# Bringing the experts' outputs to the tokens: 64-row products per batch, or 128-row products for two batches at once

## The chip, the cores and the metric

The kernel runs on one core of one Trainium2 chip. A core has a matrix engine (TensorE, shown as PE for products and PEld for weight loads), a vector engine (VectorE, DVE), a scalar engine (ScalarE, ACT), GpSimd (POOL), and DMA queues, of which SyncE's (SP) carries most transfers here. The metric is device time in microseconds (us); before the change it is 4524.53 us, the median of three runs (4481.02, 4524.53 and 4561.62). A profile of one further execution is at hand.

## The reference

The input `x` has 4 batches of 128 channels x 64 x 64 places. Four layers follow one another. Layer 0 is a state-space layer, layer 1 a hypergraph layer on the pairwise distances of 4096 places. Layers 2 and 3 treat the places as 4096 tokens of 128 channels, and each consists of an attention (linear and causal in layer 2, windowed without softmax in layer 3) and a feed-forward part with 64 experts. The change concerns the end of this feed-forward part, which occurs twice:

```
logits = einsum('bsd,ed->bse', x, gate_w) + gate_b
probs  = softmax(logits, axis=1)                  # over the 4096 tokens, per expert
vals, idx = top_k(probs over tokens, 8)           # each expert picks 8 tokens per batch
pooled = sum of the 8 picked tokens, weighted by vals      # (batch, expert, 128)
out    = expert MLP(pooled)                       # 128 -> 512 -> 128, own weights per expert
outputs[b, idx] += out[b, e] * vals               # back to the picked tokens
t = t + outputs
```

Each expert has one output row per batch, and this row, times the token's probability, is added to each of its eight tokens. Written as matrices, outputs of batch b = routeᵀ (4096 tokens x 64 experts) times the experts' outputs (64 x 128), where `route` holds the probabilities of the picked tokens and zero elsewhere.

## The kernel before

All arrays are fp32 in the parts concerned. `X` (128 partitions x 4 batches x 32 blocks x 128 channels) stays on the chip from the end of layer 1: a partition is a token's place within a block of 128 tokens. `Net.ffn` is called as the second half of layer 2, with `out=None`, and as the second half of layer 3, with the output tensor.

Within `ffn` two batches are handled together as a pair `p` (0 or 1): partitions 0 to 63 hold the 64 experts of batch 2p, partitions 64 to 127 those of batch 2p+1. So `route[p]` is 128 rows x 4096 tokens, `dens[p]` is one divisor per row, and `outT` holds all experts' outputs with channels in the partitions. The stages, in order:

1. Gate: layernorm of the tokens, transposes, logits (L970, L973, L976), and for each pair the eight largest logits per row, the exponentials and `route` (L980 to L990).
2. Pooling by products with the transposed `route` (L997 to L1011).
3. Experts, four at a time, sixteen groups: weights arrive over SP's queue in transfers of 1 MB (L947, L950) into a ring of two, products L1025, L1027, L1035, L1040, and the turn of the outputs L1048, L1049.
4. The experts' outputs are turned so that experts are in the partitions (L1057), the last layer's bias is added (L1059) and the softmax's divisor is applied (L1060). The result is `ob`, 128 rows x 128 channels, one for each pair.
5. The outputs are brought to the tokens. The loops run over the pair p, the chunk c of 512 tokens and the half r, that is the batch 2p+r.

In step 5 the call of layer 2 makes, for each (p, c, r), four products (L1071). In each, the weights are `route[p][rows, 128 tokens]` and the moving operand is `obs[p][rows, :]`, where `rows` are the 64 rows of the half r. The four results fill one PSUM tile of 128 x 512, and VectorE adds it to `X` (L1072). The call of layer 3 works the other way round, since the output has channels in the partitions. For each (p, c, r) four products with the identity (L1078) turn `X` into a PSUM tile of 128 channels x 512 tokens, and a fifth (L1082), with `obs[p][rows, :]` as weights and `route[p][rows, 512 tokens]` moving, adds the experts' part to it. ScalarE (r = 0) or VectorE (r = 1) copies the tile (L1087), and SP stores it (L1088).

The PSUM tiles of step 5 carry the tag `ps` in a pool with two buffers for each tag, so two of them exist at a time. `ob` comes from the pool `wp` with one buffer for each tag. Each engine runs its own instructions in order; a scheduler has put them in order when the kernel was built, and semaphores join the engines. After the first `ffn` comes `attn3`, which starts with layernorm statistics of `X` (L700 and L705 to L712), loads Wq, Wk and Wv (L845) and turns them (L846), and works with products of 128 rows throughout (L867, L870, L876, L896, L905).

Of the kernel before, what the change touches and what calls it, by code (L numbers as in the profile page):

```python
# [7 lines left out]
F32 = mybir.dt.float32  # L8
# [3 lines left out]
ALU = mybir.AluOpType  # L12
# [4 lines left out]
P = 128  # L17
# [6 lines left out]
E = 64  # L24
# [14 lines left out]
class Net:  # L39
# [871 lines left out]
    def ffn(self, name, out=None):  # L911
# [4 lines left out]
        nc, tc, a, X = self.nc, self.tc, self.a, self.X  # L916
# [3 lines left out]
        with ExitStack() as ctx:  # L920
            wp = ctx.enter_context(tc.tile_pool(name="fw", bufs=1))
# [4 lines left out]
            ps = ctx.enter_context(tc.tile_pool(name="fps", bufs=2, space=PSUM))  # L926
# [7 lines left out]
            b2 = wp.tile([P, P], F32, tag="b2", name="b2")  # L934
# [20 lines left out]
            route, dens = [], []  # L955
            for p in range(B // 2):
                lg = big.tile([P, N], F32, tag="lg", name="lg")
                zs = [[big.tile([P, 4, P], F32, tag="z", name="zf", bufs=17) for r in range(2)] for c in range(NCH)]
                for c in range(NCH):
                    pl = ps.tile([P, CH], F32, tag="ps", name="ps_l")  # L960
                    for r in range(2):
# [4 lines left out]
                        pt = ps.tile([P, 4, P], F32, tag="tr", name="ps_t")  # L966
                        for i in range(4):
                            j = 4 * c + i
# [25 lines left out]
                for c in range(NCH):  # L994
                    pt = ps.tile([P, 4, P], F32, tag="tr", name="ps_rt")
# [4 lines left out]
                    for i in range(4):  # L1000
                        j = 4 * c + i
                        for r in range(2):
                            nc.tensor.matmul(  # L1003
                                pp[r * E : (r + 1) * E, :], rt[:, i, r * E : (r + 1) * E], zs[c][r][:, i, :],
                                start=j == 0, stop=j == NB - 1,
# [3 lines left out]
                pt = ps.tile([P, P], F32, tag="tr", name="ps_pt")  # L1009
# [9 lines left out]
            for q in range(NG // 4):  # L1019
                po = aps.tile([P, 4, P], F32, tag="acc", name="ps_eo")  # L1020
                for k in range(4):
# [4 lines left out]
                    for i in range(EG):  # L1026
                        nc.tensor.matmul(  # L1027
                            ph[i * M : (i + 1) * M, :], pooled[:, (g * EG + i) * B : (g * EG + i) * B + M], w1[:, i, :],
                            start=False, stop=True, skip_group_check=True,
# [3 lines left out]
                    pt = ps.tile([P, 4, P], F32, tag="tr", name="ps_hT")  # L1033
# [4 lines left out]
                    for c in range(4):  # L1038
                        for i in range(EG):
                            nc.tensor.matmul(  # L1040
                                po[i * M : (i + 1) * M, k, :], hT[:, c, i * M : (i + 1) * M], w2[:, i, c, :],
                                start=c == 0, stop=c == 3, skip_group_check=True,
# [3 lines left out]
                pt = ps.tile([P, 4, P], F32, tag="tr", name="ps_oT")  # L1046
# [7 lines left out]
            obs = []  # L1054
            for p in range(B // 2):
                pt = ps.tile([P, P], F32, tag="tr", name="ps_ot")
                nc.tensor.transpose(pt, outT[:, 2 * p : 2 * p + 2, :].rearrange("p b e -> p (b e)"), self.ident)  # L1057
                ob = wp.tile([P, P], F32, tag=f"ob{p}", name="ob")
                nc.vector.tensor_tensor(ob, pt, b2, ALU.add)  # L1059
                nc.vector.tensor_scalar(ob, ob, dens[p], None, ALU.mult)  # L1060
                obs.append(ob)
            for p in range(B // 2):
                for c in range(NCH):
                    for r in range(2):
                        b, rows = 2 * p + r, slice(r * E, (r + 1) * E)
                        x = X[:, b, 4 * c : 4 * c + 4, :]
                        if out is None:
                            po = ps.tile([P, 4, P], F32, tag="ps", name="ps_f")
                            for i in range(4):
                                cs = slice((4 * c + i) * P, (4 * c + i + 1) * P)  # L1070
                                nc.tensor.matmul(po[:, i, :], route[p][rows, cs], obs[p][rows, :], start=True, stop=True)  # L1071
                            nc.vector.tensor_tensor(x, x, po, ALU.add)  # L1072
                        else:

                            sl = slice(c * CH, (c + 1) * CH)
                            po = ps.tile([P, CH], F32, tag="ps", name="ps_f")
                            for i in range(4):
                                nc.tensor.matmul(  # L1078
                                    po[:, i * P : (i + 1) * P], x[:, i, :], self.ident,
                                    start=i == 0, stop=False, skip_group_check=True,  # L1080
                                )
                            nc.tensor.matmul(  # L1082
                                po, obs[p][rows, :], route[p][rows, sl], start=False, stop=True,
                                skip_group_check=True,
                            )
                            o = tp.tile([P, CH], F32, tag="s", name="of")
                            (nc.vector.tensor_copy if r else nc.scalar.copy)(o, po)  # L1087
                            nc.sync.dma_start(out[b, :, sl], o)  # L1088
# [62 lines left out]
```

## Time and profile before

| | us |
|---|---|
| median of three runs | 4524.53 |
| the profiled execution | 4506.08 |
| its span | 4504.3 |
| layers 0 and 1, to the last stretch with the scan (0 to 2860) | 2860 |
| rest of layer 1, and attention of layer 2 (2860 to 3695) | 835 |
| first ffn: gate and pooling (3695 to 3825) | 130 |
| first ffn: experts (3825 to 3917.8) | 92.8 |
| first ffn: outputs to the tokens (3917.8 to 3964.5) | 46.7 |
| attention of layer 3 (3964.5 to 4195) | 230.5 |
| second ffn: gate and pooling (4195 to 4327) | 132 |
| second ffn: experts (4327 to 4434.2) | 107.2 |
| second ffn: outputs to the tokens, and the store (4434.2 to 4504.3) | 70.1 |

Over the span PE is busy for 82%, VectorE for 69%, GpSimd for 54%, ScalarE for 44%. These are averages over stages that are limited by different engines. A product in fp32 leaves two records on PE, each with its own weight load on PEld. A record's duration includes the time in which the next one is already running, so the sum of durations is more than the busy time, and the step from one start to the next is what a stream of products costs. "64*128" ahead of a shape says that the product uses 64 rows and 128 columns of the array. PEclk is the clock that TensorE was granted, as a share of the full one. In a list of groups the figures after the bar are busy time, mean duration of one in ns, the idle time of the engine just before, and what ended that idle time.

### The profile page before, as it was taken

What the parts mean: (1) busy time and instruction counts of PE and PEld (TensorE: products, weight loads), DVE (VectorE), ACT (ScalarE), POOL (GpSimd) and SP (SyncE); (2) the same over time, 40 slices, a digit from 0 to 9 for tenths busy, and PEclk for the clock granted to TensorE, in tenths of its full rate; (3) what the DMA queues carried; (4) which work ended last, traced back from release to release, by engine and by line L of the source; (5) the groups of instructions that cost most, each with busy time, mean ns of one, the idle gap of its engine ahead of it and who ended that gap; (6) DMA issues with size and microseconds to landing.
All of it is one profiled execution on the core that took longest, in us unless ns stands there. A gap on an engine that the chain in (4) does not pass through costs nothing. (4 is left out here: it accounts for less than half of the span.)

```text
span 4504.3 us, 50176 instructions
## 1 busy us (share of the span) xinstructions
PE 3713.7 (82%) x17975; PEld 2095.2 (47%) x17975; DVE 3124.2 (69%) x5140; ACT 1981.6 (44%) x3104; POOL 2415.8 (54%) x1182
## 2 busy tenths in 40 slices
PE   6887768888887888887878888899977995899778
PEld 2333233345433434543434454456535763578435
DVE  5888889997668999666999866453118985287621
ACT  4655554456445445644544564213225643022221
POOL 5999889887777888677888877300021000000000
PEclk8988878999998899998889999999988997789878
DMA  3455544454464445455455535312250000800044
GB/s 102 155 150 150 143 114 139 124 148 132 126 189 114 125 130 154 122 151 164 113 132 138 153 107 169 119 61 77 76 200 31 1 2 6 297 2 1 2 172 166
DMA packets 261741, 524.36 MB, mean 116 GB/s; under 512 B 21706, under 2 KB 24306, under 8 KB 261490
## 3 DMA queue, kind: packets, MB, share of 16 engines
q1 hardware_dynamic: 250194, 501.78, 37.9%
q10 hardware_dynamic: 11296, 19.37, 1.3%
q8 instruction: 142, 2.33, 0.2%
q14 instruction: 109, 0.89, 0.1%
HBM read 443.47 MB, written 77.59 MB: 116 GB/s over the span
## 5 line engine op out<-in xcount | busy, mean ns | idle before, releaser
L284 POOL TENSOR_TENSOR db<-dx,bt 128x1024 f32<-128x1024 f32 x512 | 1203.0, 2353 | 331.7 <-DVE hs L302 214.6
L302 DVE TENSOR_TENSOR_SCAN hs<-hs,carry,db 128x512 f32<-128x512 f32 x812 | 1035.2, 1282 | 177.5 <-ACT hs L296 95.2
L296 ACT ACTIVATE hs<-dl,A 128x512 f32<-128x512 f32 x1024 | 706.6, 692 | 740.6 <-DVE ho L312 687.1
L497 PE MATMUL ps_g<-xn 128*128 128x512 f32 x1152 | 602.5, 654 | 99.8 <-DVE inc L500 74.3
L319 POOL TENSOR_TENSOR ho_s<-ho_s,ho 128x1024 f32<-128x1024 f32 x288 | 677.1, 2351 | 13.8 <-DVE ho L312 13.1
L312 DVE TENSOR_TENSOR ho<-hs,bt 128x1024 f32<-128x1024 f32 x464 | 563.2, 1214 | 1.6
L520 PE MATMUL ps_ed<-xs,inc 128*128 128x258 f16 x4096 | 513.6, 286 | 18.3 <-ACT inc L513 8.6
L520 PEld LDWEIGHTS <-inc 128*128 128x128 fp8e4 x4096 | 417.8, 102 | 134.6 <-issue 60.6
L500 DVE SCALAR_TENSOR_TENSOR inc<-ps_g,hcl,hb 128x512 fp8e4<-128x512 f32 x576 | 420.3, 736 | 36.7 <-PE ps_g L497 20.9
L497 PEld LDWEIGHTS ps_g<-xn 128*128 128x128 f32 x1152 | 216.0, 204 | 416.6 <-DVE inc L500 182.9
L340 PE MATMUL ps_y<-ho,cst 128*128 128x512 f32 x512 | 274.0, 678 | 108.9 <-POOL ho L308 91.5
L620 PE MATMUL ps_v<-inc_v,es 128*128 128x512 fp8e4 x1536 | 343.1, 383 | 19.2 <-DMA bt<-bcd 17.3
L620 PEld LDWEIGHTS <-es 128*128 128x128 f16 x2048 | 202.7, 99 | 288.9 <-issue 64.1
L513 ACT CAST inc<-ps_t 128x512 fp8e4<-128x512 f32 x448 | 232.1, 600 | 94.5 <-PE ps_t L509 94.3
L222 PE MATMUL ps_c<-xt,wc 128*128 128x512 f32 x512 | 234.9, 613 | 12.6 <-DVE inc L500 6.8
L340 PEld LDWEIGHTS ps_y<-ho,cst 128*128 128x128 f32 x512 | 105.1, 214 | 269.0 <-POOL ho L308 122.6
L526 ACT COPY ed<-ps_ed 128x129 f32<-128x129 f32 x128 | 34.0, 266 | 383.7 <-PE ps_ed L520 383.7
L527 DVE TENSOR_TENSOR ed<-ps_ed,ed 128x129 f32<-128x129 f32 x128 | 36.6, 286 | 211.8 <-ACT ed L526 208.8
L302 DVE TENSOR_TENSOR_SCAN hs<-hs,db 128x512 f32<-128x512 f32 x116 | 141.2, 1223 | 53.6 <-POOL db L284 42.6
L536 POOL TENSOR_TENSOR ed<-ed,rdeg 128x512 f32<-128x512 f32 x32 | 33.3, 1039 | 250.7 <-DVE rdeg L532 250.7
L222 PEld LDWEIGHTS ps_c<-xt,wc 128*128 128x128 f32 x512 | 99.8, 198 | 140.2 <-issue 119.2
L509 PE MATMUL ps_t<-ident,strip 128*128 128x128 fp8e4 x1344 | 115.1, 227 | 51.4 <-ACT inc L513 16.9
(262 smaller groups left out, 5785.5 us busy)
## 6 DMA issues: line engine op xcount, KB each, us to landing
bt<-bcd SPq DMA_DIRECT2D x512, 512.0 KB
inc<-inc SPq DMA_DIRECT2D x192, 256.0 KB
inc_v<-inc SPq DMA_DIRECT2D x96, 512.0 KB
w<-in_L_ffn_weight SPq DMA_DIRECT2D x32, 1024.0 KB
w2f<-in_L_ffn_weight SPq DMA_DIRECT2D x32, 1024.0 KB
strip<-inc SPq DMA_DIRECT2D x84, 256.0 KB
x<-x ACTq DMA_DIRECT2D x32, 256.0 KB
xn<-x SPq DMA_DIRECT2D x32, 256.0 KB
```

The costliest lines, as they stand in the source:

```text
L222: nc.tensor.matmul(s["ps"][h], wc[:, h, j, :], xt[:, j : j + T], start=j == 0, stop=j == 3)
L284: nc.gpsimd.tensor_tensor(db, s["dx"], bc(s["bt", n][:, 0, :], 2), ALU.mult)
L296: act(nc.scalar.activation(hs[:, k, :], s["dl"][:, k, :], AF.Exp, scale=A[:, k, n : n + 1]))
L302: nc.vector.tensor_tensor_scan(to[:, h, :], hs[:, h, :], db[:, h, :], init, ALU.mult, ALU.add)
L312: nc.vector.tensor_tensor(ho, hs, ct, ALU.mult)
L319: nc.gpsimd.tensor_tensor(s["sum", n // G], s["sum", n // G], ho, ALU.add)
L340: nc.tensor.matmul(s["y"][h], self.ident, t[:, h, :], start=False, stop=n == DS - 1 and k == len(terms) - 1,)
L497: nc.tensor.matmul(pq, xn[v // 4][:, v % 4 * P : (v % 4 + 1) * P], xn[c], start=True, stop=True)
L500: nc.vector.scalar_tensor_tensor(inc[:, v, :], pq, hc[:, v : v + 1], hb, ALU.subtract, ALU.is_gt, saturate=False)
L513: later(1, lambda: act(nc.scalar.copy(inc[:, v, :], pt, saturate=False)))
L520: nc.tensor.matmul(pe[:, : 2 * P + 2], inc[:, v, i * P : (i + 1) * P], xs[:, v, :], start=v == 0, stop=v == NB - 1,)
L620: nc.tensor.matmul(pv, es[:, e, k, :], inc[:, e, :], start=e == 0 and k == 0, stop=e == NB - 1 and k == 1,)
```

## The change

`ob` becomes twice as wide: 128 rows x 2 x 128. Its two column blocks belong to the two batches of the pair. Rows 0 to 63 are filled in block 0 only and rows 64 to 127 in block 1 only; GpSimd sets the tile to zero first. The bias and the divisor are applied to each half by instructions of 64 rows.

In the call of layer 2 each product now takes all 128 rows of `route[p]` for 128 tokens as weights and the whole `ob` (256 columns) as moving operand, so that it yields both batches of the pair side by side; the zeros keep the batches apart. A PSUM tile holds 2 blocks of tokens x 2 batches x 128 channels, and one addition on VectorE adds it to `X` of both batches. In the call of layer 3 the fifth product takes block r of `ob` with all 128 rows as weights and all 128 rows of `route[p]` moving; the rows of the other batch meet zeros. The names of the lines behind the change move by seven: L1088 becomes L1095, for example.

```diff
             for p in range(B // 2):
                 pt = ps.tile([P, P], F32, tag="tr", name="ps_ot")
                 nc.tensor.transpose(pt, outT[:, 2 * p : 2 * p + 2, :].rearrange("p b e -> p (b e)"), self.ident)
-                ob = wp.tile([P, P], F32, tag=f"ob{p}", name="ob")
-                nc.vector.tensor_tensor(ob, pt, b2, ALU.add)
-                nc.vector.tensor_scalar(ob, ob, dens[p], None, ALU.mult)
+                ob = wp.tile([P, 2, P], F32, tag=f"ob{p}", name="ob")
+                nc.gpsimd.memset(ob, 0.0)
+                for r in range(2):
+                    rows = slice(r * E, (r + 1) * E)
+                    nc.vector.tensor_tensor(ob[rows, r, :], pt[rows, :], b2[rows, :], ALU.add)
+                    nc.vector.tensor_scalar(ob[rows, r, :], ob[rows, r, :], dens[p][rows, :], None, ALU.mult)
                 obs.append(ob)
             for p in range(B // 2):
                 for c in range(NCH):
                     for r in range(2):
-                        b, rows = 2 * p + r, slice(r * E, (r + 1) * E)
-                        x = X[:, b, 4 * c : 4 * c + 4, :]
                         if out is None:
-                            po = ps.tile([P, 4, P], F32, tag="ps", name="ps_f")
-                            for i in range(4):
-                                cs = slice((4 * c + i) * P, (4 * c + i + 1) * P)
-                                nc.tensor.matmul(po[:, i, :], route[p][rows, cs], obs[p][rows, :], start=True, stop=True)
+                            j = 4 * c + 2 * r
+                            po = ps.tile([P, 2, 2, P], F32, tag="ps", name="ps_f")
+                            for i in range(2):
+                                nc.tensor.matmul(
+                                    po[:, i, :, :].rearrange("p r c -> p (r c)"), route[p][:, (j + i) * P : (j + i + 1) * P],
+                                    obs[p].rearrange("p r c -> p (r c)"), start=True, stop=True,
+                                )
+                            x = X[:, 2 * p : 2 * p + 2, j : j + 2, :].rearrange("p r i c -> p i r c")
                             nc.vector.tensor_tensor(x, x, po, ALU.add)
                         else:
+                            b = 2 * p + r
                             sl = slice(c * CH, (c + 1) * CH)
                             po = ps.tile([P, CH], F32, tag="ps", name="ps_f")
                             for i in range(4):
                                 nc.tensor.matmul(
-                                    po[:, i * P : (i + 1) * P], x[:, i, :], self.ident,
+                                    po[:, i * P : (i + 1) * P], X[:, b, 4 * c + i, :], self.ident,
                                     start=i == 0, stop=False, skip_group_check=True,
                                 )
                             nc.tensor.matmul(
-                                po, obs[p][rows, :], route[p][rows, sl], start=False, stop=True,
-                                skip_group_check=True,
+                                po, obs[p][:, r, :], route[p][:, sl], start=False, stop=True, skip_group_check=True
                             )
```

## The prediction

> **What bounds the kernel now.** I read the stage table first (the span cut by hand at the stage borders), then the groups of the two stages that the change touches, then their order in time. Columns of the first view: busy time and instructions of PE, PEld, DVE, ACT and POOL, the granted clock, the DMA share, GB/s. Rows: all of layers 0 and 1 up to their ends; the product stage of the first ffn; attn3; the last stage.
>
> ```profile
> core 0: us, PE busy (x) PEld busy (x) DVE busy (x) ACT busy (x) POOL busy (x), PEclk, DMA share, GB/s
> 0.00:2860.00 2860.00, 2321.75 (x9116) 1160.69 (x9117) 2309.89 (x2791) 1491.00 (x2253) 2336.59 (x1100) 0.90 0.49 138
> ...
> 3917.80:3964.50 46.70, 45.89 (x256) 44.78 (x256) 22.20 (x35) 0.00 (x0) 0.00 (x0) 0.50 0.22 82
> 3964.50:4195.00 230.50, 222.12 (x1433) 184.87 (x1434) 179.19 (x690) 54.14 (x93) 0.00 (x0) 0.97 0.01 2
> ...
> 4434.20:4504.30 70.10, 65.42 (x304) 38.17 (x304) 11.29 (x18) 9.36 (x16) 0.00 (x0) 0.98 0.32 121
> ```
>
> The change can act in 46.7 + 70.1 = 117 us, 2.6% of the span; nothing in the other 97% is edited. Both stages keep PE busy, the first at **half clock for its whole length**, the second at full clock.
>
> ```profile
> L1071 PE MATMUL ps_f<-ob,lg 64*128 64x128 f32 x256 | 45.9, 438 | 0.6 <-DVE ob L1060 0.6
> L1078 PE MATMUL ps_f<-cst,X 128*128 128x128 f32 x256 | 37.7, 292 | 0.7 <-ACT of L1087 0.7
> L1082 PE MATMUL ps_f<-lg,ob 64*128 64x512 f32 x64 | 34.8, 641 | 0.7 <-DVE ob L1060 0.7
> L1072 DVE TENSOR_TENSOR X<-X,ps_f 128x512 f32<-128x512 f32 x32 | 22.0, 687 | 24.5 <-PE ps_f L1071 24.5
> ```
>
> Each product leaves two PE records (256 for 128 calls). DVE waits for PE, so PE, or the ring of two PSUM tiles around it, sets the pace. In order of time:
>
> ```profile
> 3920.00 0.69 DVE L1072 TENSOR_TENSOR X<-X,ps_f 128x512 f32<-128x512 f32 x1 [1.97 <-PE ps_f L1071]
> 3921.02 0.69 DVE L1072 TENSOR_TENSOR X<-X,ps_f 128x512 f32<-128x512 f32 x1 [0.34 <-PE ps_f L1071]
> 3922.86 0.69 DVE L1072 TENSOR_TENSOR X<-X,ps_f 128x512 f32<-128x512 f32 x1 [1.15 <-PE ps_f L1071]
> ...
> 4438.28 1.16 PE L1078 MATMUL ps_f<-cst,X 128*128 128x128 f32 x8
> 4439.37 0.29 PEld L1082 LDWEIGHTS ps_f<-lg,ob 64*128 64x128 f32 x2
> 4439.37 1.12 PE L1082 MATMUL ps_f<-lg,ob 64*128 64x512 f32 x2
> 4440.42 0.97 PEld L1078 LDWEIGHTS ps_f<-cst,X 128*128 128x128 f32 x8 [0.76 <-issue]
> ```
>
> First stage: two tiles leave every 3922.86 - 3920.00 = 2.86 us. One tile takes 3920.00 - 3917.89 = 2.1 us from its first product to the add, the add 0.69, and PE then starts again: 2.86. So the ring of two is the bound, one tile per row half at a time. Last stage: a group (four identity products and one of `route`) takes 4440.42 - 4438.28 = 2.14 us.
>
> [...] The trace has only 0.5 and 1.0, but does not agree that being busy is enough: these 64-row products fill 45.89 of 46.70 us and stay at 0.50. I infer that an array half unused doesn't count as busy enough. [...] the two halves overlap, but only as far as the ring lets them. [...] PEld idles 0.76 us at each return from 64 to 128 rows, its releaser only "issue".
>
> **Part 1, the first ffn's products.** Removed: 256 records of 64 rows x 128 columns. Added: 128 records of 128 rows x 256 columns. The price is from the same form in attn3 at full clock, and that of 512 columns from layer 1:
>
> ```profile
> 3982.24 1.89 PE L876 MATMUL ps_kv<-wT,zT 128*128 128x256 f32 x8
> ...
> 2917.16 3.60 PE L497 MATMUL ps_g<-xn 128*128 128x512 f32 x8
> 2920.59 0.95 PE L469 MATMUL ps_hc<-ones,sq 128*128 128x1 f32 x8
> ```
>
> Eight records of 256 columns take 1.89 us; less the last one's own 0.38, seven steps of 0.216. At half clock I double it, 0.43. A tile is now four records: 4 x 0.216 = 0.86 us of PE. Its round in the ring at full clock: weights 0.11 (half of the 0.19 row is exposed), three steps 0.65, the last record 0.38, 0.08 to the add, the add 0.69, 0.05 back to PE: 1.95 us, against 2 x 0.86 = 1.73 us of PE for two tiles. The ring stays the bound, with 1.95 us per two tiles; sixteen rounds are 31.2 us. At half clock PE would be: 8 x 0.427 = 3.41 us per two tiles.
>
> The stage starts at half clock. How long it stays there is taken from attn3, whose first transposes and products of 128 rows start at 3972.0 and have the full clock from 3976.3: 4.3 us[...]. I take 5, in which 1 - 1.95/3.41 = 43% is lost: 2.1 us. With 0.9 us for the last add, 34.2 us against 46.6 (3917.9 to 3964.5): **-12.4 us**. With the clock up at once -14.5; never up, 16 x 3.41 + 0.9 = 55.5, +8.9. The next stage gains nothing: PE idles about 7 us there until layernorm's statistics are done.
>
> The add writes two batches in one instruction with an inner run of 128: as many elements as the 687 ns row. I take 687; up to 800, still in the ring, would be 16 x 0.11 = 1.8 us; a gain is excluded, as the count is equal.
>
> **Part 2, the last stage.** The 32 products of `route` keep 512 columns (64 records) but have 128 rows[...]. L497 gives 512 columns a step of (3.60 - 0.59) / 7 = 0.43 us, and the switch there from 512 columns to L469 costs nothing: 2920.59 - 2917.16 = 3.43 = 8 x 0.429. Of the 1.16 us of eight identity records 0.11 is an exposed weight load and 0.275 the last record; seven steps of 0.111 remain. A group becomes 8 x 0.111 + 2 x 0.429 = 1.75 us against 2.14, so 0.39 less. Thirty steady groups (the first two have their identity part done before the experts' end): **-11.7 us**. Bounds: 0 [...], and not above -12.5 for all 32. What is late next: ACT and DVE empty a tile in 0.59 and 0.69 us, in turn, with two tiles in 3.5 us; the stores, 256 KB per 1.75 us or 150 GB/s, where the trace has moved over 300. So PE stays the bound.
>
> **Part 3, what is added or moved.** DVE builds `ob` with 4 + 4 instructions of 64 rows instead of 2 + 2 of 128, per ffn. They last about the same (279 and 276 ns, stepping by 0.2); the first product waits for four in place of three: +0.2 per ffn, **+0.4 us**; bounds 0 and +1. Behind them on DVE stand only the adds or copies that need the products. Four POOL memsets of 128x256: the trace has POOL 128x512 at 1.3 us, so 0.7 each as an estimate; POOL is empty (0.00) and the experts' phase of 93 and 107 us hides them. Without that cover both together cost 1.4 us per ffn. On the SP queue the loads of Wq, Wk and Wv move behind three 1 MB weight loads. DMA is quiet after 3930, so they land by about 3931 instead of earlier, and their readers (L846) come after the last add, then at 3952. Nothing; if they came late, each us is one us. PE's order is otherwise the same.
>
> **Sum.** -12.4 - 11.7 + 0.4 = -23.7 us. The profiled execution took 4506.1 us (span 4504.3 and 1.8 around it), 18 below the median of 4524.5. So 4482 for an execution like the profiled one, and 4524.5 - 23.7 = 4501, say **4500**, for the median.
>
> **Rivals.** (a) Likeliest, both gains: 4500; 0.74. (b) The clock stays at half in the first stage: half of the moving columns are zeros, and `route` is nearly empty besides (8 of 4096 tokens per expert), which may count as little work. Against: L1003 has the same emptiness in its 128-row weights, and the clock rises at 4256 in the middle of it. +8.9 - 11.7 + 0.4 = -2.4: 4522; 0.13. (c) The 0.39 us in the last stage [...] stay: -12.0: 4512; 0.06. (d) Ends slower: the clock falls to half in both stages, by the same zeros. A last-stage group is then 8 x 0.213 + 2 x 0.853 = 3.41 us, 30 x (3.41 - 2.14) = +38; with +8.9 and +0.4 4572. It decides from two such groups on, for each costs 1.66 us more than forecast and (b) has only 2.4 in hand. Against: its identity operand is as empty today and has clock 1.00; 0.03. The rest, 0.04, is a price wrong by more than its bounds.
>
> **How the numbers follow.** All cases but (d) lie within 22 us, less than the 81 us between the three runs before (4481 to 4562), so scatter sets the range: 35 us for one run, some 25 for a median of three, the same again for the median I start from, 44 us either way at 8 in 10: **4456 to 4544**. It takes in (b) and (c) and leaves out (d). About 2%, 90 us, is what a measurement of this kernel can tell from no change. Faster by more would need three quarters of both stages gone: 0.04, all scatter. Slower by more: 0.03. Within: 0.93.
>
> **What would show it.** Right: clock 1.00 in the first stage [...], its length 33 to 36 us, DVE's adds in pairs every 1.95 us; in the last stage a group every 1.75 us and no "issue" idle ahead of the identity's weight loads. Wrong: clock 0.50 and pairs every 3.4 us; groups still 2.14 us; another stage's length changed by more than a few us.

## The result, and the profile after

| | before | after |
|---|---|---|
| median of 22 runs each, us | 4509.41 | 4485.68 |
| lowest and highest, us | 4481.02 to 4577.25 | 4459.38 to 4496.88 |
| span of the profiled execution, us | 4504.3 | 4488.1 |

The ratio is 0.9945, with a 95% interval of 0.9926 to 0.9963: the changed kernel is faster by about half a per cent, less than the 2% named in the prediction. The ratio leaves out executions that lie more than 1.5% above the fastest of their kernel, and so a part of the upper group of runs that is explained below.

The stage table of the profile after, with the columns as in the prediction (time, busy time and instructions of PE, PEld, DVE, ACT and POOL, granted clock, DMA share, GB/s). The first row is the product stage of the first ffn, the second attn3, the third the last stage from its first product of `route`:

```profile
3932.90:3965.80 32.90, 32.15 (x128) 22.89 (x128) 23.10 (x37) 0.00 (x0) 0.00 (x0) 0.95 0.27 102
3965.80:4195.60 229.80, 222.25 (x1433) 184.85 (x1434) 179.16 (x689) 54.14 (x93) 0.00 (x0) 0.99 0.01 2
4429.50:4488.10 58.60, 54.64 (x304) 38.80 (x304) 12.46 (x21) 9.38 (x16) 0.00 (x0) 1.00 0.39 144
```

The first product stage takes 32.9 us in place of 46.6 and has clock 0.95 in place of 0.50. The last stage takes 58.5 us (4429.58 to 4488.1) in place of 70.0 (4434.29 to 4504.3), counted from the first product of `route`. The groups of products:

```profile
L1086 PE MATMUL ps_f<-cst,X 128*128 128x128 f32 x256 | 33.8, 275 | 0.0
L1086 PEld LDWEIGHTS ps_f<-cst,X 128*128 128x128 f32 x256 | 33.4, 191 | 14.6 <-issue 13.9 <-ACT of L1094 0.7
L1090 PE MATMUL ps_f<-lg,ob 128*128 128x512 f32 x64 | 32.7, 595 | 1.1 <-DVE ob L1064 1.1
L1074 PE MATMUL ps_f<-ob,lg 128*128 128x256 f32 x128 | 32.1, 410 | 1.3 <-DVE ob L1064 1.3
```

PE has no gap left in the last stage but the wait for `ob` (1.1 us). The 13.9 us of "issue" ahead of the identity's weight loads are no loss: PE itself has no idle time there (0.0 in its row). They are less than before the change (22.0), but not gone, as the prediction had it. In order of time, the adds of the first stage, then two groups of the last:

```profile
3936.40 0.69 DVE L1079 TENSOR_TENSOR X<-X,ps_f 128x512 f32<-128x512 f32 x1 [0.73 <-PE ps_f L1074]
3937.26 0.69 DVE L1079 TENSOR_TENSOR X<-X,ps_f 128x512 f32<-128x512 f32 x1 [0.18 <-PE ps_f L1074]
3938.31 0.69 DVE L1079 TENSOR_TENSOR X<-X,ps_f 128x512 f32<-128x512 f32 x1 [0.36 <-PE ps_f L1074]
...
4433.26 1.05 PE L1086 MATMUL ps_f<-cst,X 128*128 128x128 f32 x8
4434.15 1.02 PE L1090 MATMUL ps_f<-lg,ob 128*128 128x512 f32 x2
4435.01 1.05 PE L1086 MATMUL ps_f<-cst,X 128*128 128x128 f32 x8
```

Two tiles leave every 3938.31 - 3936.40 = 1.91 us, and a group of the last stage takes 4435.01 - 4433.26 = 1.75 us.

The two profiled executions differ by 16.2 us, which is less than what the two stages gained. Cut at four marks (the first search for the eight largest, L980; the first turn of the outputs, L1057; the last L980; the last L1057) the difference is:

| stretch | before | after | difference |
|---|---|---|---|
| start to the first L980 | 3724.3 | 3724.8 | +0.5 |
| to the first L1057 (pooling and experts of the first ffn) | 192.3 | 206.1 | +13.8 |
| to the last L980 (products to the tokens, attn3, second gate) | 374.4 | 360.7 | -13.7 |
| to the last L1057 (pooling and experts of the second ffn) | 142.4 | 136.7 | -5.7 |
| to the end (last stage) | 70.9 | 59.8 | -11.1 |

The stretches with the edited code give -24.8 us. The two experts' stretches run the same instructions as before. In the eight profiles of changed kernels that follow, all with the wide `ob`, they take 188 to 203 and 127 to 144 us; in three more executions of the kernel before the first takes 193 to 206 and the second 135 to 139. So +13.8 and -5.7 are taken as their scatter, and not as the change's doing.

### The profile page after: what moved, and what is told of

It is laid out like the page before. It is cut to its first block, busy times and chain, and to the rows that moved or that the text cites. A ratio compares the mean times of both kernels' runs of the same rounds, so it can differ in the third digit from the quotient of the medians.

```text
span 4488.1 us, 49942 instructions
## 1 busy us (share of the span) xinstructions
PE 3697.9 (82%) x17847; PEld 2077.2 (46%) x17847; DVE 3128.4 (70%) x5148; ACT 1981.9 (44%) x3104; POOL 2417.1 (54%) x1186
## 5 line engine op out<-in xcount | busy, mean ns | idle before, releaser
L319 POOL TENSOR_TENSOR ho_s<-ho_s,ho 128x1024 f32<-128x1024 f32 x288 | 677.6, 2353 | 13.9 <-DVE ho L312 13.3
```

Source lines behind the costliest of these rows:

```text
L319: nc.gpsimd.tensor_tensor(s["sum", n // G], s["sum", n // G], ho, ALU.add)
```

## The experiments

### One part alone

The first kernel keeps the 64 rows in the last stage:

```diff
-                                po, obs[p][:, r, :], route[p][:, sl], start=False, stop=True, skip_group_check=True
+                                po, obs[p][r * E : (r + 1) * E, r, :], route[p][r * E : (r + 1) * E, sl], start=False, ...
```

> Only the first ffn's products are changed; the last stage takes 64 rows of the wide ob as before. If the two gains are independent, as the sum in the prediction takes them: first product stage 33 us with clock 1.00 [...], last stage about 70 us with a group every 2.14 us, and the weight loads of the identity products idle 0.76 us ahead of each group. If instead the clock of the last stage or its gaps depend on what the first stage did, the group time differs from 2.14.

Measured: 4545.39 us for one execution, while the kernel before took 4497.5 on the same chip. The stage table of this kernel, for the two stages:

```profile
3920.80:3953.80 33.00, 32.22 (x128) 22.97 (x128) 23.09 (x37) 0.00 (x0) 0.00 (x0) 0.95 0.27 100
4417.60:4543.60 126.00, 121.62 (x304) 68.90 (x304) 12.44 (x21) 9.38 (x16) 0.00 (x0) 0.51 0.18 67
```

The first stage has its whole gain (33.0 us). The last one took 126 us in place of 70, at half clock from 4419.0 to its end. A group took 4.0 us (4427.49 - 4423.48):

```profile
4423.48 2.07 PE L1086 MATMUL ps_f<-cst,X 128*128 128x128 f32 x8
4425.49 2.07 PE L1090 MATMUL ps_f<-lg,ob 64*128 64x512 f32 x2
4427.49 2.07 PE L1086 MATMUL ps_f<-cst,X 128*128 128x128 f32 x8
```

So the expectation missed: a last stage with 64-row products can run at half clock to its end. Whether this was an accident of one execution is asked below.

The second kernel takes the 64 rows in the first ffn only:

```diff
-                                    po[:, i, :, :].rearrange("p r c -> p (r c)"), route[p][:, (j + i) * P : (j + i + 1) * P],
-                                    obs[p].rearrange("p r c -> p (r c)"), start=True, stop=True,
+                                    po[:, i, :], route[p][rows, cs], obs[p][rows, r, :], start=True, stop=True
```

(with four calls per tile and the addition for one batch, as before the change).

> Only the last stage is changed; the first ffn's products take 64 rows as before. [...] a group every 1.75 us, no gap at the change from 512 to 128 columns, last stage 58 to 59 us. First product stage 46 to 47 us at clock 0.50, as before. Rival (the gap comes from the wide ob or from the clock, not from the switch of 64 to 128 rows): the group time would stay at 2.14.

Measured: 4496.39 us. The stage table of this kernel, the first stage cut where the clock changes:

```profile
3915.00:3919.30 4.30, 2.18 (x29) 1.47 (x23) 1.85 (x7) 0.58 (x1) 0.00 (x0) 1.00 0.60 201
3919.30:3964.70 45.40, 44.64 (x253) 43.45 (x251) 22.74 (x36) 0.00 (x0) 0.00 (x0) 0.50 0.21 75
...
4434.50:4494.60 60.10, 56.20 (x304) 39.43 (x304) 12.43 (x21) 9.37 (x16) 0.00 (x0) 0.96 0.38 141
```

Groups of the last stage come every 1.75 us (4439.79, 4441.54, 4443.30), so the gap of 2.14 - 1.75 = 0.39 us goes with the 64 rows of the last stage and needs nothing of the first. The first stage shows more than was asked. It began at full clock at 3918.6, the clock fell at 3919.3, and it stayed at half for 45 us, with PE busy for 44.64 of 45.40 us. The fall itself says little of the 64 rows: from 3915.9 to 3919.3 PE was busy for 1.77 us only, since it had waited for `ob`, and an execution with all rows, shown with the third kernel, lost the clock after a like stretch. And the last stage of this kernel, with all rows, lost the clock too, at 4434.8, but had it back at 4438.2; it took 60.1 us and not the 58 to 59 expected.

### What the clock goes by

The third kernel keeps the four calls of 128 columns per tile and one batch at a time, but with all rows, the other batch's meeting the zeros of `ob`. If the clock goes by how much of the array is in use, as the prediction inferred from the 0.50 of the first stage before, it should be full here:

```diff
-                                    po[:, i, :, :].rearrange("p r c -> p (r c)"), route[p][:, (j + i) * P : (j + i + 1) * P],
-                                    obs[p].rearrange("p r c -> p (r c)"), start=True, stop=True,
+                                    po[:, i, :], route[p][:, cs], obs[p][:, r, :], start=True, stop=True
```

> The first ffn's products keep 128 calls of 128 columns, one batch each, as before, but take all 128 rows, with zeros in ob against the other batch. Theory [...]: clock 1.00 [...], one tile 8 records of 0.111 us, two tiles every 2.0 us, stage 34 us. Rival (the wider stream of 256 columns, fewer records, raised the clock): clock stays at 0.50, 8 records of 0.213 us per tile, stage 55 us or more. Rival (zeros count as no work): the same 55 us.

Measured: 4475.0 us, first stage 32.2 us, two tiles every 1.94 us (adds at 3922.53, 3924.47, 3926.40).

```profile
3919.10:3951.30 32.20, 31.27 (x256) 29.81 (x256) 23.23 (x38) 0.00 (x0) 0.00 (x0) 1.00 0.31 114
```

The stage began at full clock and kept it for 32 us, where the one with 64 rows stayed at half for 45 us. The width of 256 columns was not needed for that, and zeros on half the rows were no obstacle (clock 1.00 for these 32.2 us). That this stage kept a clock which the second kernel lost at its start doesn't yet show it, for a kernel with all rows lost the clock there as well. In another execution of a kernel with all rows in this stage (that of the first experiment, executed again, first product at 3926.4), PE was busy for 1.40 of the 3.30 us ahead, and the clock fell at 3926.7:

```profile
3923.40:3926.70 3.30, 1.40 (x8) 0.93 (x9) 1.80 (x7) 0.11 (x1) 0.00 (x0) 1.00 0.80 246
3926.80:3930.10 3.30, 3.30 (x10) 2.59 (x9) 1.58 (x5) 0.00 (x0) 0.00 (x0) 0.50 0.96 327
3930.20:3933.50 3.30, 3.30 (x16) 2.35 (x14) 2.37 (x4) 0.00 (x0) 0.00 (x0) 1.00 1.05 407
```

It was back after 3.4 us. The difference is in the return: with all rows the clock came back, after 3.4 us here and 3.0 in the changed kernel; with 64, mostly of one half at a time, it stayed at 0.50 for the second kernel's 45.4 us.

The fourth kernel goes back to 64 rows, but alternates the halves call by call, into two tiles of different tags, so that both row groups are in use at once. If the clock goes by the rows in use at a time, it should be full here too:

```diff
+                            pos = [ps.tile([P, 4, P], F32, tag=t, name="ps_f") for t in ("ps", "tr")]
+                            for i in range(4):
+                                for k in range(2):
+                                    rows = slice(k * E, (k + 1) * E)
+                                    nc.tensor.matmul(pos[k][:, i, :], route[p][rows, cs], obs[p][rows, k, :], ...)
```

> The first ffn's products take 64 rows as before, but the two halves alternate call by call into two PSUM tiles of different tags, four tiles in all, so that both row groups run at once all the time. [...] clock 1.00, a pair of tiles bound by the two adds, 1.4 to 1.5 us, stage 24 us. If products of 64 rows never count as busy: clock 0.50, a pair 8 x 0.213 = 1.7 us, stage 28 to 30 us. If row groups don't run at once: 55 us at half clock or 28 us at full clock.

Measured: 4476.77 us, first stage 21.9 us. The second row is this stage in a further execution (4470.72 us), which began at full clock:

```profile
3919.80:3941.70 21.90, 20.12 (x256) 17.46 (x256) 20.71 (x38) 0.00 (x0) 0.00 (x0) 0.91 0.44 160
3918.80:3939.60 20.80, 18.97 (x256) 16.03 (x256) 20.64 (x38) 0.00 (x0) 0.00 (x0) 1.00 0.49 180
```

Two rounds of its weight loads in order of time, each for a pair of tiles (start, length, engine and line, and at the end of the line the idle time before and what ended it):

```profile
3924.96 0.97 PEld L1078 LDWEIGHTS ps_f<-ob,lg 64*128 64x128 f32 x16 [0.30 <-DVE X L1081]
3926.15 0.97 PEld L1078 LDWEIGHTS ps_f<-ob,lg 64*128 64x128 f32 x16 [0.22 <-DVE X L1081]
```

This stage began at half clock, with products of 64 rows, and had the full clock from 3923.7. Together with the second and third kernel this shows that the clock didn't go by PE's busy time alone: products mostly of one half at a time (the second kernel: 16 records of 0.213 us, 3.41 in all, in a round of 2.85), PE busy for 44.64 of 45.40 us, left it at half, and both halves at once, PE busy for 20.12 of 21.90 us, had it back after 3.9 us. All rows had it back too, in the changed kernel after 3.0 us. Whether the 64-row products of the kernel before would keep a clock that is full is not shown: in all five profiles that have them in the first stage it was at half 0.7 us after the start or sooner. A pair of tiles takes 3926.15 - 3924.96 = 1.19 us, twice 0.60 of additions: now VectorE is the bound, busy for 20.71 of 21.90 us, and the stage is 11 us shorter than in the changed kernel.

### The ring of two

```diff
-                            po = ps.tile([P, 2, 2, P], F32, tag="ps", name="ps_f")
+                            po = ps.tile([P, 2, 2, P], F32, tag=("ps", "tr")[r], name="ps_f")
```

> The changed kernel with one edit: the PSUM tiles of the first ffn's products alternate between two tags, so that four exist in place of two. If the ring of two is what the stage waits for (the prediction: 1.95 us per two tiles; the profile of the changed kernel: 1.91): two tiles every 8 x 0.216 = 1.73 us, PE the bound, stage 29.5 to 30.5 us if it starts at half clock, against 32.9. If the ring is no bound: 1.91 and 32.9 as before.

Measured: additions every 0.86 us (3930.16, 3931.02, 3931.89), thus 1.73 us for two tiles, and a first stage of 30.2 us (3921.4 to 3951.6), also begun at half clock.

```profile
3921.40:3951.60 30.20, 29.41 (x128) 25.33 (x128) 23.09 (x37) 0.00 (x0) 0.00 (x0) 0.95 0.33 118
```

The ring was the bound in the changed kernel, by 0.18 us per two tiles.

### The two ways of a last stage with 64 rows

The kernel with the first part alone was run more often:

> The same kernel as the first experiment (64 rows in the last stage), timed. Theory (a last stage with 64-row products has two ways to run: a clock that is full when it begins stays full, one that has dropped to half never comes back): times in two clusters some 55 us apart, about 4485 to 4500 and 4540 to 4560, and a median with a wide interval. Rival (the half clock in the first look was a disturbance of that one run): all within 30 us, 10 to 14 us below the kernel before.

Measured, 22 runs: nine from 4471 to 4507 us, thirteen from 4532 to 4577, median 4540.38, against 4518.53 in 43 runs of the kernel before beside it. So the first part alone shows no gain in the overall median: thirteen of its 22 runs lie in the upper group, of the kernel before 18 of 43. Within the groups the gain is there: the medians are 4491.3 against 4504.9 and 4548.8 against 4564.2, thus 14 and 15 us lower. The two groups are there, and the 126 us of the first experiment were no accident. One sentence of the expectation fell: the profiled execution of this run had lost the clock at 4421.7, in its first groups, and had it back at 4425.1, after which the stage ran as in the profile before. So a lost clock came back while the stage began, 3.4 us after its fall; once the steady groups of 4.0 us ran at half clock, it did not come back in any of the profiles here. While the stage begins both halves are at work at once: in this execution the first four records of 512 columns passed in 2.14 us, mostly at half clock, where one half at a time would take about 3.4 (an estimate, 4 x 0.853).

Three more executions of the kernel before were profiled:

> The kernel before, looked at again, to see where its upper cluster of times (4530 to 4580 us) comes from. Theory: an execution above 4530 us has its last stage at half clock, with a group every 4.0 us and about 126 us in all; one below 4525 has a group every 2.14 us and 70 us; the first product stage takes 46 to 47 us in both. Rival (the clusters come from the experts' phases): the last stage is 70 us in all of them, and the experts' phases differ by 50 us.

> The kernel before, one more execution, with the same two theories: a time above 4530 us goes with a last stage of 126 us, one below 4525 us with 70 us; or the last stage is 70 us in each and the experts' phases make the difference.

> The kernel before, a third execution, with the same two theories: a time above 4530 us goes with a last stage of 126 us, one below 4525 us with 70 us; or the last stage is 70 us in each and the experts' phases make the difference.

Measured: 4559.17, 4571.85 and 4510.64 us. The stage tables of the first and the third execution, the first product stage and the last stage of each:

```profile
3921.10:3967.50 46.40, 45.59 (x256) 44.48 (x256) 22.23 (x34) 0.00 (x0) 0.00 (x0) 0.50 0.24 88
4431.50:4557.40 125.90, 121.30 (x304) 68.56 (x304) 11.22 (x17) 9.38 (x16) 0.00 (x0) 0.51 0.18 67
```

```profile
3925.50:3971.60 46.10, 45.34 (x256) 44.73 (x256) 22.17 (x34) 0.00 (x0) 0.00 (x0) 0.51 0.25 87
4438.90:4508.90 70.00, 65.38 (x304) 38.12 (x304) 11.17 (x17) 9.38 (x16) 0.00 (x0) 0.98 0.32 121
```

The second execution, 4571.85 us, had 126.8 us in its last stage. The experts' phases don't make the difference: ahead of the last stage they took 136, 135 and 139 us. So in the profiled executions the upper group of the kernel before is the last stage at half clock: 126 us against 70. Of the 43 runs of the kernel before that stand beside the later experiments, 18 lie above 4530 us (median 4564.2) and 25 below (median 4504.9), without a wide gap between them (4521 to 4531), and no execution of it between 4511 and 4559 us was profiled. Of the changed kernel's 22 none is above 4497. With all rows in the last stage the clock was lost at its beginning in some executions as well (the second and fourth kernel above), and came back each time: within 3.4 us in these two, and after 10.2 us in the kernel with four tiles, whose clock fell at 4412.7, ahead of the stage.

Which way an execution goes seems to hang on its moment. In the traces before and after, the granted clock changes only at points that lie whole multiples of 3.41 us apart (212 stretches in each, to within 8 ns), and the falls and returns given above for other executions are 3.4 and 10.2 us apart. Counted in such steps from each profile's own changes, the first such point after the last stage's first product of `route` came, in the six profiles with 64-row products there, 0.2, 0.4, 1.3, 2.0, 2.6 and 2.8 us behind it. The clock fell there in the first four and was kept in the last two; of the four, only the one at 0.4 had it back. With all rows, in five other profiles, it fell at 0.2 and 0.3 us and came back, and was kept at 1.3, 1.9 and 2.2. These are single executions, and nothing was built to move that point, so this is a reading and not shown. An estimate from the figures above says why both ways can last: a steady group uses all rows for 0.89 us (8 x 0.111) and half of them for 0.86 (2 x 0.429), together worth 1.32 us of all rows. That is 62% of 2.14 us at full clock, and about twice as much, some 65%, of 4.00 us at half clock. If the clock goes by the share of rows in use, which no run here tests by itself, the two states look alike, and neither need end by itself.

### Both halves at once in both stages

The fourth kernel was run more often, and one was added that treats the last stage likewise: eight identity products into two tiles, then the two 64-row products of the two halves side by side.

```diff
+                            for k in range(2):
+                                rows = slice(k * E, (k + 1) * E)
+                                nc.tensor.matmul(
+                                    pos[k], obs[p][rows, k, :], route[p][rows, sl], start=False, stop=True, skip_group_check=True
+                                )
```

> The kernel with both row groups at once in the first ffn (21.9 us there in the first look) and 128 rows in the last stage, timed: 11 us below the changed kernel, thus 35 us or 0.8% below the kernel before by medians, ratio 0.992 of the medians, and one cluster of times only, since its last stage uses all rows.

Measured, 17 runs: median 4472.82 us (4455.28 to 4488.23), ratio 0.9929, interval 0.9906 to 0.9952. One group only, as expected; 13 us below the changed kernel by medians. These come from separate sets of runs, and the interval overlaps with the changed kernel's (0.9926 to 0.9963); what is clear is the first stage, 21.9 and 20.8 us against 32.9.

> As the kernel with both row groups at once, and in the last stage the two halves in pairs: eight identity products into two tiles, then the two 64-row products, which lie in different row groups, with four PSUM tiles. [...] both products of 512 columns at once, 16 x 0.111 + 0.86 + 0.39 = 3.0 us for two groups against 3.5 in the changed kernel, last stage 51 us against 58.5, total 18 us below the changed kernel. Without overlap of the two products 3.9 us for two, last stage 65 us. [...] half clock and over 90 us.

Measured, 11 runs: median 4465.85 us (4448.94 to 4479.23), ratio 0.9891, interval 0.9855 to 0.9927, 20 us below the changed kernel by medians of separate sets. The last stage, and then its products in order of time; two groups take 3.04 us:

```profile
4403.80:4455.40 51.60, 47.16 (x297) 32.37 (x296) 11.45 (x18) 9.36 (x16) 0.00 (x0) 0.96 0.44 164
...
4408.32 2.05 PE L1090 MATMUL ps_f<-cst,X 128*128 128x128 f32 x16
4410.30 1.13 PE L1096 MATMUL ps_f<-lg,ob 64*128 64x512 f32 x4
4411.36 2.05 PE L1090 MATMUL ps_f<-cst,X 128*128 128x128 f32 x16
```

Four records of 512 columns, two for each half, pass in 4411.36 - 4410.30 = 1.06 us, where two take 1.05 in the kernel before: the halves overlap fully, and the 0.39 us of the switch between 128 and 64 rows (both ways together) are paid once for two groups. The zeros of the changed kernel bought the clock (0.95 and 1.00 in its two stages) and the 0.39 us of each group, but every row of the other batch is streamed; with both halves in use at once the clock was 0.92 and 0.96 in the two stages without that. In this execution too the clock was at half when the last stage began, and it came back at 4406.6, 3.4 us after it had fallen.

## Why the prediction was right, and what it missed

**The first ffn's products: right, by its own mechanism.** Forecast 34.2 us, measured 32.9. The round of the ring was put at 1.95 us and is 1.91, and the half clock at the start was put at 5 us and was 3.0 (3932.9 to 3935.9); both err on the same side. That all rows bring the clock up, which the prediction inferred from one stage that stayed at half, is shown by the changed kernel itself (0.50, then 1.00 after 3.0 us), with the second, third and fourth kernel against it. "An array half unused" was too wide in one point: the fourth kernel's products have 64 rows each, and with both halves running at once the clock was 1.00 from 3923.7 on. Rivals (b) and (d), in which zeros count as no work, are excluded by the changed kernel and the third.

**The last stage: right in a clock that is full.** A group was forecast at 1.75 us and takes 1.75; -11.7 was forecast and -11.5 measured from the first product on. The second kernel shows that it is the rows and not the first stage, so rival (c) falls. The last kernel, in which one switch serves two groups and the 0.39 us are paid once for both, ties them to the switch. The named sign fared worse than the cost: "no 'issue' idle ahead of the identity's weight loads" was to show the cost of the switch gone, and 13.9 of 22.0 us stayed, although PE has no idle time there. The group's length is the sign to go by.

**The building of `ob`: a term too small.** Forecast +0.4 us for both. From the first instruction on DVE to the first product it was 0.75 us in the first ffn and 0.73 in the second (3917.14 to 3917.89, 4433.56 to 4434.29); now it is 1.39 and 1.07: +1.0 together, at the upper bound. The step of two such instructions of 64 rows is 0.3 us, not the 0.2 taken from those with 128 rows. And only the first ffn's product waits for four of them; the last stage's first needs one half of `ob` and waits for three. The zeroing cost nothing that shows: the four instructions on GpSimd took 0.33 us each, not 0.7, and ran at 3691.8 and 4197.1, long before the experts.

**The weights of attn3: wrong in the time, right in the cost.** Wq was to land by about 3931. In the changed kernel SP issues it only at 3965.11, after the last product, and PE waits 1.97 us for it. SP stood at a semaphore for 33.6 us ahead of it, against 1.4 before. What holds it back was not tried; that the wider `ob` shifts the tiles behind it in the memory is a guess. The wait costs nothing that shows: VectorE makes layernorm's statistics meanwhile, and the first transposes follow the last addition's end by 7.0 us, against 7.5 before.

**The sum.** -23.7 us was forecast; the edited stretches of the two profiled executions give -24.8, the medians of 22 runs -23.7. The last agreement is partly luck, for the medians mix two groups. The forecast of 4500 for the median itself was 14 us high (measured 4485.68), because it started from the middle one of three runs, 4524.5, where 22 runs have 4509.41.

**What it missed.** The prediction took the 81 us between the three runs before as scatter that would stay. They are not scatter of one kind: the highest of the three, 4561.62, lies in the upper group, which the three further profiles tie to a last stage at half clock. Rival (d) had a last stage at half clock, at somewhat too low a price (3.41 us for a group, measured 4.00; by that estimate the switch costs 0.59 there, not nothing), but gave zeros as the cause and put it on the changed kernel, when it was the kernel before that had it, in two of its four profiled executions. The profile before showed the lucky execution only. The change takes this away: of the 22 runs of the kernel before beside it, 7 lie above 4530 us (median 4561.6) and 15 below (median 4502.8), so it gains some 76 us against the upper group and 17 against the lower one, and its range is 38 us wide in place of 96. Against the lower group the profiles had promised 24 to 25; the remaining 7 to 8 us are less than the scatter of the experts' phases and stay open.

## What to carry to other kernels

In this kernel products on half of the array's rows cost more than the idle half: a stage of them ran at clock 0.50 with PE busy for 45.89 of 46.70 us, and one that mixes them with 128-row products took 70 us in one execution and 126 in another. Look at the granted clock of each stage and not at busy time alone, and where a kernel's runs fall into two groups, profile one of each. Filling the rows with zeros was one cure (first stage 46.6 to 32.9 us); running the two halves at the same time, with four PSUM tiles for it, was the better one here (20.8 and 21.9 us), and is worth trying where the data allow it.

## What the runs showed of the hardware

- 64-row products mostly of one half at a time, PE busy for 44.64 of 45.40 us: the clock stayed at 0.50 (second kernel). 64-row products in both row groups at once: clock back to 1.00 after 3.9 us (fourth kernel). Products of 128 rows, half of them against zeros: back after 3.0 us (changed kernel).
- The granted clock was 0.50 or 1.00 and changed only at points whole multiples of 3.41 us apart, in the traces before and after.
- A mix of 128-row and 64-row products (at half clock 2.0 us of each in a group of 4.0) ran at either clock: the same stage took 70.1 us at 0.98 and 125.9 us at 0.51, in two executions of the kernel before.
- The switch between 128 and 64 rows cost 0.39 us there and back at full clock (a group of 2.14 us in place of 1.75); at half clock a group took 4.00 us where its columns alone need 3.41 (an estimate, 8 x 0.213 + 2 x 0.853).
- Additions of 128x512 from PSUM lasted 0.69 us each but followed one another every 0.60 us when none had to wait (11 of them in 6.66 us, fourth kernel).
